# Restormer block on one core: the order of all instructions computed from other durations and margins

## The chip, the cores and the metric

The kernel runs on one core of a Trainium2 chip. A core has five engines that run side by side, each with its own in-order queue of instructions: TensorE (PE: matrix products and transposes, results into PSUM), VectorE (DVE), ScalarE (ACT), GpSimd (POOL) and SyncE (SP, which here only starts transfers). Sixteen DMA engines move data; transfers that add to what stands at their goal are started by GpSimd here. The metric is the device time of one launch in microseconds (us).

## The reference

One block of a Restormer-like network on x of shape (16, 128, 96, 96): 16 images, 128 channels, 96 x 96 pixels, float32. Attention is over channels (8 heads of 16 channels), then a feed-forward part with a 3 x 3 depthwise convolution over 512 hidden channels:

```python
x_hwc = x.transpose(0, 2, 3, 1)
xn1 = _layernorm(x_hwc, ln1_w, ln1_b)          # over the 128 channels of each pixel
q, k, v = xn1 @ wq.T, xn1 @ wk.T, xn1 @ wv.T   # split into heads, q and k l2-normed over the pixels
attn = softmax(einsum('bhcn,bhdn->bhcd', q, k) * HEAD_DIM ** -0.5)
attn_out = einsum('bhcd,bhdn->bhcn', attn, v) @ wp.T
x = x + attn_out
xn2 = _layernorm(x, ln2_w, ln2_b)
h1 = einsum('bchw,oc->bohw', xn2, w_in)        # 128 -> 512 channels
h2 = depthwise_conv_3x3(h1, w_dw)              # padding 1
h3 = gelu(h2)
x = x + einsum('bchw,oc->bohw', h3, w_out)     # 512 -> 128 channels
```

## The kernel before

**Tiles and stages.** An image is cut into 8 bands of 12 rows (`BR`), a band into 3 units of 4 rows (`UR`, 384 pixels); there are 128 bands in all. Channels lie on the 128 partitions. For each image the work goes through these stages:

1. Norm a (first layer norm, `norm(i, False, ...)`). A band of x is loaded by SP (`load`, L546 to L554). TensorE transposes four blocks of 128 pixels into one PSUM tile (`forth`, L624), VectorE takes the statistics of them (`stats`, L631, two instructions), GpSimd makes variance plus epsilon (`variance`, L638) and its power -0.5 (`power`, L642), ScalarE scales into zT (`scaled`, L678), TensorE adds the block to the Gram matrix (`gram`, L692) and transposes back (`back`, L730), and ScalarE puts the result into a ring of 144 rows in SBUF called xn (`place`, L736).
2. `attention` (L755 to L877): some fifteen small steps, from the Gram matrix to one 128 x 128 matrix that does attention and projection at once.
3. `x2` (L565 to L605): TensorE applies that matrix (`mix`, L572), ScalarE evicts (`mixed`, L581), an adding transfer by GpSimd adds x from HBM (`add_x`, L584), SP stores the sum to the output (`keep_x2`, L587).
4. Norm b (second layer norm): the same lines as norm a, with a VectorE instruction between power and scaling (`shift`, L646, it writes nb), ScalarE's scaling in L682, and without the Gram matrix.
5. `conv_job` (L884 to L972), one job for each band and chunk of 128 hidden channels: TensorE computes the hidden rows (`hidden`, L905), ScalarE copies them to h1 (`kept`, L908), VectorE does six of the eight outer taps of the convolution (`tap`, L929, some 1152 elements each, two tensors in SBUF as inputs), ScalarE makes the products of two taps (`product`, L922) and adding transfers by GpSimd put them together (`add_products`, L936), ScalarE keeps two rows for the next band (`halo`, L900) and applies GELU (L940). In 7 of 15 bands the fourth chunk's convolution is done by TensorE instead (`by_matmuls`, L994, GELU in L1000).
6. `ffn_out` (L1009 to L1056): TensorE's output product (L1018), ScalarE's eviction (L1030), and an adding transfer by GpSimd to the output (L1034); for the last two bands VectorE adds (L1025) and SP stores.

**What sets the order.** No instruction is issued where it stands in the source. Each step is given to a planner (`Plan`, L59 to L203) with `op`: its engine, its time on that engine, a place, what it reads and writes, and the time after which another engine may use its result (`result`). `Plan.order` plays all engines at once: whenever an engine is idle in its model, it takes the ready step with the smallest place whose buffers are free. Places are counted in convolution jobs and come from the loop position plus an offset for the kind of step (`at`, L346, with the table `AT`, L35; kinds that end in `_0` are image 0's). The steps are then emitted in the planned order of their starts, so this order fixes each engine's queue; on the chip only the queue's order and the waits for data and buffers remain. The planner's buffers are PSUM tiles for transposes (`tr`, 2), for products (`h`, 4 banks), for transposes back (`bk`, 1), the Gram matrix (`g`, 1), and SBUF tiles (`zT` 3, `x1` 3, `xb` 3, `pr` 5, `h3` 12).

**What the planner is told.** Times are simple formulas (L357 to L367: `t_mm`, `t_dve`, `t_act`, `t_copy`). The result of a step counts as seen by another engine after its time, a latency, and `SLACK`, 200 ns for all engines. GpSimd's variance and power are given as 1150 and 1870 ns (220 and 1010 in the early part of image 0). A transfer starts `WAIT` after its issue, or behind the transfer before it, and takes `T_ADD` (254 ns for each of 12 rows, 3048 in all) if it adds, or `T_MOVE` (133 a row, 1596) if SP starts it.

The two helpers for transfers, and the step that the planner makes of one, read:

```python
def add(p, f, r, w):
    op("POOL", 950, p, f, r, w, 1400 + SLACK, dma=T_ADD)
def move(p, f, r, w, ns):
    op("SP", 60, p, f, r, w, 900 + SLACK, dma=ns)
...
if o[8]:
    self.dma = max(time + ns + WAIT[engine], self.dma) + o[8]
    result = own = self.dma + result - time
```

## Time and profile before

| | |
|---|---|
| Median of 3 runs | 4153.88 us (4144.19 to 4156.89) |
| The profiled execution: its time | 4147.01 us |
| its span | 4145.3 us |
| TensorE's granted clock, mean | 0.997 |
| Instructions | 52245 |
| ScalarE busy | 3656.0 us (88%) |
| GpSimd busy | 2602.5 us (63%) |
| Transfers | 828.63 MB, mean 200 GB/s |

The page of a profile shows one execution: how long each engine was busy, the chain of work that ended last, and groups of equal instructions. A group's line reads: line of the code, engine, operation, what it writes <- what it reads, shapes, count | busy time in us, mean ns of one | idle time of the engine just before them, and what ended most of it. A line of waits reads: who waited <- for whom: us in total, times, longest. PEld are TensorE's weight loads, which overlap its products. A busy time is a union, so overlapping instructions count once, and the mean of one can be longer than busy time divided by count. A line of stretches gives, for each part of the span, the busy time of each engine with its number of instructions, the granted clock, the busy share of the DMA engines and what they moved. A line of transfers gives the KB of each and the median us from issue to landing.

### The profile page before, as it was taken

What the parts mean: (1) busy time and instruction counts of PE and PEld (TensorE: products, weight loads), DVE (VectorE), ACT (ScalarE), POOL (GpSimd) and SP (SyncE); (2) the same over time, 40 slices, a digit from 0 to 9 for tenths busy, and PEclk for the clock granted to TensorE, in tenths of its full rate; (3) what the DMA queues carried; (4) which work ended last, traced back from release to release, by engine and by line L of the source; (5) the groups of instructions that cost most, each with busy time, mean ns of one, the idle gap of its engine ahead of it and who ended that gap; (6) DMA issues with size and microseconds to landing.
All of it is one profiled execution on the core that took longest, in us unless ns stands there. A gap on an engine that the chain in (4) does not pass through costs nothing.

```text
span 4145.3 us, 52245 instructions
## 1 busy us (share of the span) xinstructions
PE 4060.7 (98%) x17287; PEld 2654.1 (64%) x17287; DVE 4040.2 (97%) x4446; ACT 3656.0 (88%) x7158; POOL 2602.5 (63%) x2358
## 2 busy tenths in 40 slices
PE   8999999999999999999999999999999999999999
PEld 7666666666666666666666666666666566666555
DVE  7999999999999999999999999999999999999998
ACT  5998988998989899888889889998899888999885
POOL 4767567664766656567566666766667666675442
PEclk9999999999999999999999999999999999999999
DMA  4999999999999999999999999999999899999997
GB/s 139 200 196 208 197 208 201 209 210 198 209 201 206 204 202 209 205 202 202 202 205 202 209 202 209 212 203 207 204 206 210 184 210 203 202 200 189 197 182 151
DMA packets 205519, 828.63 MB, mean 200 GB/s; under 512 B 23744, under 2 KB 25152, under 8 KB 205248
## 3 DMA queue, kind: packets, MB, share of 16 engines
q0 software_dynamic: 165744, 673.46, 84.9%
q1 hardware_dynamic: 37152, 151.01, 9.9%
q8 instruction: 138, 2.26, 0.2%
q10 hardware_dynamic: 2352, 0.81, 0.1%
q14 instruction: 133, 1.09, 0.1%
HBM read 150.03 MB, written 149.82 MB: 72 GB/s over the span
## 4 chain that ended last, share of the span: by engine, by line
PE 63%; DVE 24%; ACT 5%; DMA 4%; POOL 3%; issue 2%; POOLq 0%; ACTq 0%; DVEq 0%
DVE h L929 21%; PE h L994 17%; PE h L1018 16%; PE h L905 13%; PE g L692 4%; PE h L572 4%; PE pB_a L730 2%; PE pT_b L624 2%; PE pT_a L624 2%; PE pB_b L730 2%; DMA h<-pr 2%; DVE st_b L631 1%; DVE st_a L631 1%; ACT pr L922 1%; DMA pr<-pr 1%
## 5 line engine op out<-in xcount | busy, mean ns | idle before, releaser
L929 DVE SCALAR_TENSOR_TENSOR h<-h,ratio,h 128x1140 f32<-128x1140 f32 (+1 forms) x2257 | 3056.8, 1383 | 1.1
L922 ACT ACTIVATE pr<-h,ratio 128x1152 f32<-128x1152 f32 (+1 forms) x900 | 1153.2, 1286 | 100.6 <-DMA h<-pr 52.8
L994 PE MATMUL h<-xn,comp 128*128 128x380 f32 (+3 forms) x3324 | 1166.9, 481 | 9.2 <-ACT h L908 5.7
L1018 PE MATMUL h<-h,woutT 128*128 128x384 f32 x3072 | 1113.8, 488 | 10.8 <-ACT h L908 6.9
L905 PE MATMUL h<-xn,winT 128*128 128x384 f32 (+3 forms) x2746 | 1052.5, 490 | 15.7 <-ACT x L581 8.2
L994 PEld LDWEIGHTS h<-xn,comp 128*128 128x128 f32 x3324 | 604.4, 191 | 355.2 <-ACT h L908 8.6
L1018 PEld LDWEIGHTS h<-h,woutT 128*128 128x128 f32 x3072 | 562.0, 191 | 350.8 <-ACT h L940 12.0
L908 ACT COPY h<-h 128x384 f32<-128x384 f32 (+2 forms) x1353 | 657.0, 521 | 73.5 <-PE h L905 53.7
L936 POOL DMA_DIRECT2D pr<-pr x450 | 427.7, 950 | 435.0 <-ACT pr L922 387.0
L936 POOL DMA_DIRECT2D h<-pr x450 | 454.2, 1009 | 368.2 <-DVE h L929 153.0
L905 PEld LDWEIGHTS h<-xn,winT 128*128 128x128 f32 x2746 | 491.2, 190 | 301.8 <-issue 29.4
L929 DVE SCALAR_TENSOR_TENSOR h<-h,ratio 128x1152 f32<-128x1152 f32 x451 | 632.8, 1409 | 6.7 <-ACT h L908 6.6
L940 ACT ACTIVATE h<-h 128x1152 f32<-128x1152 f32 x453 | 546.5, 1209 | 20.4 <-DMA h<-pr 16.0
L642 POOL TENSOR_TENSOR rstd_a<-ve_a,mhalf 128x4 f32<-128x4 f32 x288 | 551.0, 1913 | 15.0
L642 POOL TENSOR_TENSOR rstd_b<-ve_b,mhalf 128x4 f32<-128x4 f32 x288 | 531.0, 1845 | 10.9
L638 POOL TENSOR_SCALAR ve_b<-st_b 128x4 f32<-128x4 f32 x288 | 329.1, 1143 | 247.8 <-DVE st_b L631 242.5
L638 POOL TENSOR_SCALAR ve_a<-st_a 128x4 f32<-128x4 f32 x288 | 330.3, 1147 | 215.4 <-DVE st_a L631 178.6
L682 ACT ACTIVATE zT<-pT_b,nb_b,rstd_b 128x128 f32<-128x128 f32 x1132 | 433.5, 492 | 31.6 <-DVE nb_b L646 29.9
L678 ACT ACTIVATE zT<-pT_a,rstd_a 128x128 f32<-128x128 f32 x1080 | 316.8, 409 | 9.5 <-POOL rstd_a L642 9.4
L692 PEld LDWEIGHTS g<-zT 128*128 128x128 f32 x2304 | 296.1, 193 | 41.3 <-issue 2.5
L572 PE MATMUL h<-xn,mwT 128*128 128x384 f32 x768 | 310.3, 490 | 7.5 <-ACT h L908 4.3
L692 PE MATMUL g<-zT 128*128 128x129 f32 x2304 | 307.5, 276 | 0.0
(172 smaller groups left out, 3675.4 us busy)
## 6 DMA issues: line engine op xcount, KB each, us to landing
h<-pr POOLq DMA_DIRECT2D x450, 576.0 KB, 8.4
pr<-pr POOLq DMA_DIRECT2D x338, 576.0 KB, 7.4
x<-in_x_dram SPq DMA_DIRECT2D x128, 576.0 KB, 6.7
out_dram<-x SPq DMA_DIRECT2D x127, 576.0 KB, 8.1
out_dram<-out POOLq DMA_DIRECT2D x126, 576.0 KB, 7.7
x<-in_x_dram POOLq DMA_DIRECT2D x125, 576.0 KB, 8.5
pr<-pr POOLq DMA_DIRECT2D x112, 528.0 KB, 7.7
out_dram<-x SPq DMA_DIRECT2D x3, 192.0 KB, 1.9
```

What stands on the lines that cost most here:

```text
L572: nc.tensor.matmul(rows(pm), lhsT=mats[i][0], rhs=interior(i, u), start=True, stop=True)
L638: nc.gpsimd.tensor_scalar(ve, d["mv"][:, :, 2], 1.0 / C, EPS, ALU.mult, ALU.add)
L642: nc.gpsimd.tensor_tensor(rstd, d["ve"], mhalf, ALU.pow)
L692: nc.tensor.matmul(grams[i][:, : P + 1], lhsT=zt[:, :P], rhs=zt, start=(q == 0 and k == 0), stop=(q == NU * TPU // QT - 1 and k == QT - 1),)
L905: nc.tensor.matmul(rows(ph)[:, k : k + m, :], lhsT=winT[:, n, :], rhs=z, start=True, stop=True)
L908: nc.scalar.copy(window(h1_, r, e - r, 1), rows(d.pop(("ph", r))))
L922: nc.scalar.activation(d["pr", t][:, o0:o1, :], shifted(t, o0, o1), AF.Copy, scale=ratio[:, n, t : t + 1])
L929: nc.vector.scalar_tensor_tensor(h3[:, o0:o1, w0:w1], shifted(t, o0, o1, w0, w1), ratio[:, n, t : t + 1], onto, ALU.mult, ALU.add)
L936: nc.gpsimd.dma_start(out=to[:, o0:o1, :], in_=d["pr", t][:, o0:o1, :], accum_op=ALU.add)
L940: nc.scalar.activation(h3, h3, AF.Gelu)
L994: nc.tensor.matmul(d["pc"][:, o0 + k : o0 + k + m, w0:w1], lhsT=comp[:, t, :], rhs=z[:, :, w0 + dx : w1 + dx], start=(t == order[0]), stop ...
L1018: nc.tensor.matmul(rows(d["po"]), lhsT=woutT[:, n, :], rhs=h3s[g, n][:, s * UR : (s + 1) * UR, :], start=(k == 0), stop=(k == NCH - 1),)
```

## The change

No step is added or taken away, and every step computes what it did. What the planner is told is changed, and with it the order of the instructions on each engine:

- All offsets in `AT` are new.
- `SLACK` becomes a table: 910 ns behind TensorE, 200 behind VectorE and ScalarE, 0 behind GpSimd's computing steps, 150 behind an adding transfer, 950 behind one that SP starts.
- Transfers: `T_ADD` 234 a row instead of 254, `T_MOVE` 121 instead of 133; `WAIT` 700 instead of 350 for GpSimd's and 1800 instead of 1300 for the others; the issue of an adding transfer takes GpSimd 800 ns instead of 950, and the latency behind a landing is 350 instead of 1400 (adding) and 900 (SP), before the margin.
- GpSimd's computing steps: variance is 250 ns and power 1010, for all images. The planner remembers until when a tap runs on VectorE (`self.two`, the tap's end plus 35 ns; only taps are marked, by `two=True`). A GpSimd computing step that starts before that time gets the rest of it added, less 143 ns. A GpSimd step that issues a transfer does not.
- The memsets of `zeros` and the table load are planned by the common helpers, at 300 and 200 ns and 1400 ns.

```diff
@@ -33,27 +33,27 @@
 LAST_ADDS = 2
 IN_TURN = ("tr", "h3", "pr", "xb", "x1")
 AT = dict(
-    load_1=-81.8, load_2=-81.05, tables=-300.65, weights=-241.6, zeros=-79.35, load_a=-132.3, forth_a=-3.95,
-    stats_a=-119.7, variance_a=57.65, power_a=43.15, scaled_a=67.75, gram=-0.3, back_a=-131.9, place_a=-4.05,
-    attention=-126.85, mix=-6.1, residual=-100.05, mixed=-72.7, add_x=-106.2, forth_b=-1.2, stats_b=-57.55,
-    variance_b=-94.65, power_b=108.15, shift_b=-68.05, scaled_b=71.3, back_b=-38.35, place_b=67.85, evicted=4.6,
-    add_out=-80.65, halo=139.4, hidden=2.8, kept=-53.4, products=2.05, add_last=-216.85, tap=8.1,
-    add_first=-80.7, gelu=650.75, conv=2.7, conv_gelu=7.9, out=6.35, add=107.4, store=112.35, mix_0=-6.7,
-    residual_0=15.25, mixed_0=37.15, add_x_0=-22.1, gram_0=6.6, forth_a_0=-278.4, forth_b_0=-3.6,
-    stats_a_0=37.95, stats_b_0=-249.6, scaled_a_0=-24.3, scaled_b_0=34.15, back_a_0=-105.15, back_b_0=-197.05,
-    place_a_0=-82.25, place_b_0=38.25, shift_b_0=0.7, late=-240.45, store_x2=23.55, store_x2_0=14.25,
-    variance_a_0=-76.6, variance_b_0=30.05, power_a_0=-132.1, power_b_0=29.1, attention_0=-126.55,
-    load_a_0=-197.15,
+    load_1=-125.15, load_2=-188.5, tables=-11.6, weights=105.75, zeros=-270.15, load_a=-127.15, forth_a=-3.95,
+    stats_a=-128.3, variance_a=70.6, power_a=-352.75, scaled_a=390, gram=0.2, back_a=-88.4, place_a=-42.05,
+    attention=-122.25, mix=-6.1, residual=-130.75, mixed=-134.85, add_x=-93.4, forth_b=-1.35, stats_b=-0.75,
+    variance_b=-212.2, power_b=50.85, shift_b=-88.2, scaled_b=99.6, back_b=-12.4, place_b=96.6, evicted=5.8,
+    add_out=-269.35, halo=538.7, hidden=2.8, kept=-49.15, products=2.05, add_last=-420.95, tap=9.15,
+    add_first=-34.25, gelu=905.05, conv=2.7, conv_gelu=8.7, out=6.35, add=-76.25, store=-175.9, mix_0=-5.4,
+    residual_0=-85.05, mixed_0=-4.8, add_x_0=56.3, gram_0=-182.1, forth_a_0=51.65, forth_b_0=-3.7,
+    stats_a_0=8.9, stats_b_0=-80.85, scaled_a_0=-176.8, scaled_b_0=1.1, back_a_0=-4.5, back_b_0=-114.85,
+    place_a_0=-35.45, place_b_0=80.15, shift_b_0=-69, late=129.95, store_x2=-48.1, store_x2_0=-109.6,
+    variance_a_0=286, variance_b_0=110.1, power_a_0=-128.05, power_b_0=15.9, attention_0=-253.7,
+    load_a_0=-278.85,
 )
 STEP = dict(scaled=0.3, hidden=0.1, products=0.5, tap=0.166, conv=1.6, conv_tap=0.03, out=0.8, out_part=0.05)
-SLACK = 200
+SLACK = dict(PE=910, DVE=200, ACT=200, POOL=0, ADD=150, MOVE=950)
 NORM1_END = 6.0
 EARLY = 5
-WAIT = dict(POOL=350, SP=1300, ACT=1300)
+WAIT = dict(POOL=700, SP=1800, ACT=1800)
 T_WEIGHTS = 3000
-T_VARIANCE = 1150
-T_POWER = 1870
-T_ADD, T_MOVE = 254 * BR, 133 * BR
+T_VARIANCE = 250
+T_POWER = 1010
+T_ADD, T_MOVE = 234 * BR, 121 * BR
 
 
 class Plan:
@@ -69,8 +69,9 @@
         self.slot = {}
         self.ops, self.writer, self.readers, self.users = [], {}, {}, {}
         self.dma = 0.0
-
-    def op(self, engine, ns, place, work, reads, writes, result, own=None, dma=0):
+        self.two = 0.0
+
+    def op(self, engine, ns, place, work, reads, writes, result, own=None, dma=0, two=False):
 
 
 
@@ -98,7 +99,7 @@
                 self.users.setdefault(t, []).append(k)
                 needs[self.users[t][0]] = True
         needs.pop(k, None)
-        self.ops.append((engine, ns, place, work, list(needs), new, result, own or result, dma))
+        self.ops.append((engine, ns, place, work, list(needs), new, result, own or result, dma, two))
 
     def order(self):
         ops, free = self.ops, self.free
@@ -162,6 +163,12 @@
             if o[8]:
                 self.dma = max(time + ns + WAIT[engine], self.dma) + o[8]
                 result = own = self.dma + result - time
+            elif engine == "POOL":
+                rest = self.two - time
+                ns, result = (ns, result) if rest <= 0 else (rest + ns - 143, rest + result - 143)
+                own = result
+            if o[9]:
+                self.two = time + ns + 35
             push(time + own, "own", k)
             push(time + ns, "idle", k)
             push(time + result, "done", k)
@@ -367,19 +374,22 @@
         return 50 + 0.832 * n
 
     def pe(ns, p, f, r, w):
-        op("PE", ns, p, f, r, w, ns + 200 + SLACK, ns)
-
-    def dve(ns, p, f, r, w):
-        op("DVE", ns, p, f, r, w, ns + 120 + SLACK, ns + 120)
+        op("PE", ns, p, f, r, w, ns + 200 + SLACK["PE"], ns)
+
+    def dve(ns, p, f, r, w, two=False):
+        op("DVE", ns, p, f, r, w, ns + 120 + SLACK["DVE"], ns + 120, two=two)
+
+    def pool(ns, p, f, r, w):
+        op("POOL", ns, p, f, r, w, ns + 33 + SLACK["POOL"])
 
     def add(p, f, r, w):
-        op("POOL", 950, p, f, r, w, 1400 + SLACK, dma=T_ADD)
+        op("POOL", 800, p, f, r, w, 350 + SLACK["ADD"], dma=T_ADD)
 
     def move(p, f, r, w, ns):
-        op("SP", 60, p, f, r, w, 900 + SLACK, dma=ns)
+        op("SP", 60, p, f, r, w, 350 + SLACK["MOVE"], dma=ns)
 
     def act(ns, p, f, r, w):
-        op("ACT", ns, p, f, r, w, ns + 150 + SLACK, ns + 150)
+        op("ACT", ns, p, f, r, w, ns + 150 + SLACK["ACT"], ns + 150)
 
     def zeros(p):
 
@@ -389,9 +399,9 @@
             nc.gpsimd.memset(t[:, r * WP :], 0.0)
 
         for t in zT_bufs:
-            op("POOL", 300, at("zeros", p - 1), lambda t=t: nc.gpsimd.memset(t[:, :, P:], 1.0), [], [("w", "ones")], 500)
+            pool(300, at("zeros", p - 1), lambda t=t: nc.gpsimd.memset(t[:, :, P:], 1.0), [], [("w", "ones")])
         for t in h1s:
-            op("POOL", 1000, at("zeros", p), lambda t=t: around(t), [], [("w", "pads")], 1200)
+            pool(300, at("zeros", p), lambda t=t: around(t), [], [("w", "pads")])
 
     def weights(p):
 
@@ -499,7 +509,7 @@
             for n in range(NCH):
                 nc.vector.tensor_scalar(v["wt"][:, n, :], v["win"][:, n, :], unit[:, n : n + 1], None, ALU.mult)
 
-        op("ACT", 1400, at("tables", p), table, [], [tables], 1500)
+        act(1400, at("tables", p), table, [], [tables])
         op("ACT", 2700, at("load_1", p), loads_1, [], [mine[1], small_1], T_WEIGHTS, dma=1000)
         op("ACT", 2300, at("load_2", p), loads_2, [], [mine[0], small_2], T_WEIGHTS, dma=1800)
         dve(1400, at("late", p), units, [small_2], [("w", "in")])
@@ -694,15 +704,14 @@
                         start=(q == 0 and k == 0), stop=(q == NU * TPU // QT - 1 and k == QT - 1),
                     )
 
-            t_variance, t_power = (T_VARIANCE, T_POWER) if not early else (220, 1010)
             trs, bt = [(key_, (name, q)) for q in qs], ("batch", (name, m))
             for q, tr in zip(qs, trs):
                 units = {t // TPU: None for t in range(q * QT, (q + 1) * QT)}
                 pe(110 * QT, at("forth" + ab, s, i), lambda q=q: forth(q), [xtok(u) for u in units], [tr])
             for j in range(QB * QT // 2):
                 dve(341, at("stats" + ab, s, i), lambda j=j: stats(j), [trs[2 * j // QT]], [bt])
-            op("POOL", t_variance, at("variance" + ab, s, i), variance, [], [bt], t_variance + 33 + SLACK)
-            op("POOL", t_power, at("power" + ab, s, i), power, [], [bt], t_power + 33 + SLACK)
+            pool(T_VARIANCE, at("variance" + ab, s, i), variance, [], [bt])
+            pool(T_POWER, at("power" + ab, s, i), power, [], [bt])
             if second:
                 dve(80, at("shift" + ab, s, i), shift, [], [bt])
             for h, (q, tr) in enumerate(zip(qs, trs)):
@@ -710,7 +719,7 @@
                 if by_dve:
                     if apart and q % 2 == 0:
                         both = [(*zt_of(k), j) for k in (q, q + 1) for j in range(2)]
-                        op("POOL", 200, at("zeros", sh), lambda q=q: zT(q), [], both, 300)
+                        pool(200, at("zeros", sh), lambda q=q: zT(q), [], both)
                     dve(by_dve * 240, at("scaled" + ab, sh, i), lambda q=q: also_scaled(q), [tr, bt], [(*zt, 0)])
                 act((QT - by_dve) * (343 if second else 250), at("scaled" + ab, sh, i), lambda q=q: scaled(q), [tr, bt], [(*zt, 1)])
                 if not second:
@@ -773,7 +782,7 @@
 
         def step(engine, ns, also=(), reads=(), writes=mine):
             def add(f):
-                op(engine, ns, s, f, [("w", "qk"), *reads], [*writes, *also], ns + 200 + SLACK)
+                op(engine, ns, s, f, [("w", "qk"), *reads], [*writes, *also], ns + 200 + SLACK[engine])
             return add
 
         wide = [("x1", ("attention", i), k) for k in range(2)]
@@ -962,7 +971,7 @@
             add(at("add_last", j), lambda t=t: add_products(t), [pr[1 + k]], [pr[0]])
         for k, t in enumerate(left):
             o0, o1 = reach(t)
-            dve(t_dve((o1 - o0) * (W if k == 0 or t % 3 == 1 else W - 1)), at("tap", j + STEP["tap"] * k), lambda t=t: tap(t), [*h1, ("w", "pads")], h3)
+            dve(t_dve((o1 - o0) * (W if k == 0 or t % 3 == 1 else W - 1)), at("tap", j + STEP["tap"] * k), lambda t=t: tap(t), [*h1, ("w", "pads")], h3, True)
         if dma_taps:
             add(at("add_first", j), lambda: add_products(dma_taps[0]), [pr[0]], h3)
         if to_halo:
```

## The prediction

> **What bounds the kernel now.** I read the head of the page first, then the chain of waits.
>
> ```profile
> span 4145.3 us, 52245 instructions
> PE 4060.7 (98%) x17287; PEld 2654.1 (64%) x17287; DVE 4040.2 (97%) x4446; ACT 3656.0 (88%) x7158; POOL 2602.5 (63%) x2358
> ...
> PE 63%; DVE 24%; ACT 5%; DMA 4%; POOL 3%; issue 2%; POOLq 0%; ACTq 0%; DVEq 0%
> ```
>
> TensorE (PE) and VectorE (DVE) both look full. To see which one cannot give way, look at the time of one instruction: taps (L929) and output products (L1018), first in the page's groups, then in the long pieces of the chain.
>
> ```profile
> L929 DVE SCALAR_TENSOR_TENSOR h<-h,ratio,h 128x1140 f32<-128x1140 f32 (+1 forms) x2257 | 3056.8, 1383 | 1.1
> L1018 PE MATMUL h<-h,woutT 128*128 128x384 f32 x3072 | 1113.8, 488 | 10.8 <-ACT h L908 6.9
> ```
> ```profile
> 4126.25 15.49 PE h L1018 x48
> ```
>
> L1018 takes 1113.8/3072 = 0.363 us of busy TensorE per instruction on the average, and 15.49/48 = 0.323 us in the last, unbroken stretch: 11% of that busy time can be squeezed. The taps have no such reserve: their records agree within the mean of 1.38 us, with 1.1 us of idle time before 2257 of them. So VectorE is the floor: 4040.2 us of work that a new order does not change, and 4145.3 - 4040.2 = 105.1 us in which it stands. (The Trainium skill, "Perfetto Trace Analysis", section "Identifying the Most-Contended Engine", says that matmul busy time misleads and weight-load time should be used; by its rule TensorE would be 64% full, not 98%, which leaves VectorE alone as the bound.) Where the 105 us lie, by stage:
>
> ```profile
> core 0: us, PE busy (x) PEld busy (x) DVE busy (x) ACT busy (x) POOL busy (x), PEclk, DMA share, GB/s
> 0.00:100.00 100.00, 86.25 (x539) 70.13 (x540) 71.22 (x193) 56.60 (x144) 46.25 (x108) 0.98 0.48 138
> 100.00:4100.00 4000.00, 3932.67 (x16618) 2559.11 (x16617) 3934.44 (x4225) 3583.53 (x6990) 2550.15 (x2244) 1.00 0.97 202
> 4100.00:4146.00 46.00, 41.73 (x133) 24.89 (x131) 34.59 (x30) 15.86 (x25) 6.08 (x7) 1.00 0.57 124
> ```
>
> 28.8 us in the first 100, 65.6 in the 4000 of the middle, and 10.7 in the 45.3 that are left. What ended the waits of the middle:
>
> ```profile
> DVE st_b L631 <- PE pT_b L624: 25.9, 31, 7.7
> DVE st_a L631 <- PE pT_a L624: 11.3, 21, 1.5
> DVE nb_b L646 <- POOL rstd_b L642: 8.3, 7, 2.0
> DVE n L828 <- PE g L822: 4.3, 8, 0.9
> DVE h L929 <- ACT h L908: 3.7, 4, 2.3
> DVE wide L800 <- ACT h L900: 2.4, 1, 2.4
> ```
>
> They are few: some 70 waits, 55.9 us in these rows. More than half is the statistics (L631) waiting for the transposes (L624). No instruction is added or removed by the change, so anything it gains comes out of these rows, the head and the tail.
>
> **The change part by part.**
>
> *Margin behind TensorE, 200 to 910 ns.* The planner now believes that another engine sees a TensorE result 0.71 us later, so statistics are put later behind their transposes, and other VectorE work (taps) in front. Without the longest wait the st_b row has 18.2 us in 30 waits, 0.61 us each, and st_a has 0.54 us each: most are shorter than the added margin. The most that it can take away is 18.2 + 11.3 + 0.7 = 30 us. It costs something too, because the planner holds PSUM banks 0.71 us longer, and TensorE already waits for banks or inputs from ScalarE:
>
> ```profile
> PE h L905 <- ACT x L581: 8.2, 9, 1.8
> PE pB_a L730 <- ACT xn L734: 7.6, 4, 6.5
> PE h L1018 <- ACT h L908: 6.9, 5, 2.9
> ```
>
> 18 such waits of another 0.71 us would be 13 us if VectorE had to follow. Between -30 and +13 I take -15: half of the gain, since the rows' mean wait is below the margin but a real delay of TensorE is not the same each time.
>
> *GpSimd's own times.* Variance and power go from fixed 1150 and 1870 ns to 250 and 1010, plus what is left of a tap that is under way, less 143 ns. The rows they must match (groups, then the record of L638 and L642):
>
> ```profile
> L642 POOL TENSOR_TENSOR rstd_a<-ve_a,mhalf 128x4 f32<-128x4 f32 x288 | 551.0, 1913 | 15.0
> L638 POOL TENSOR_SCALAR ve_a<-st_a 128x4 f32<-128x4 f32 x288 | 330.3, 1147 | 215.4 <-DVE st_a L631 178.6
> ```
> ```profile
> L638 POOL TENSOR_SCALAR ve_a<-st_a x288: 185/1262/11223, 8.0 to 3751.6; 128x4 f32<-128x4 f32 x144
> ```
> ```profile
> L642 POOL TENSOR_TENSOR rstd_a<-ve_a,mhalf x288: 996/2073/11022, 8.6 to 3753.0; 128x4 f32<-128x4 f32 x144
> ```
>
> The old constants are the means (1.147, 1.913), but with 233 ns on top; the new ones follow the pattern, a short time alone (0.185, 0.996) and about a tap more under a tap (1.262, 2.073). With a whole tap of 1.38 us left the new plan says 1.38 + 0.107 = 1.49 and 1.38 + 0.867 = 2.25 us, a little over the medians. It gains at most the 8.3 us of the nb_b row. Against it stands the maximum, 11.2 us, which no plan has:
>
> ```profile
> 3235.02 11.22 POOL L638 TENSOR_SCALAR ve_a<-st_a 128x4 f32<-128x4 f32 x1
> ```
> ```profile
> 3255.88 0.43 DVE L631 BATCH_NORM_STATS2 st_b<-pT_b 128x6 f32<-128x256 f32 x1 [7.70 <-PE pT_b L624]
> ```
> ```profile
> 3240.00:3260.00 20.00, 13.45 (x64) 9.22 (x63) 11.92 (x14) 11.64 (x25) 14.31 (x11) 0.83 0.64 124
> ```
>
> GpSimd stood there for 11.2 us, eight taps by their mean; the scaling behind it, then the PSUM buffers, then the transposes came late, and VectorE lost 20 - 11.92 = 8.1 us. One more such place is +8. I take -4, half of the row. (The Trainium skill, "SBUF — State Buffer", section "A bandwidth-pool intuition that's wrong (but worth ruling out)", has GpSimd blocked until the end of the VectorE instruction plus about 115 ns. The new planner computes much the same; by it no record would pass 1.38 + 0.115 + 0.996 = 2.5 us, and the loss at 3255 could not be. The trace has 11.2 us, so the measurement decides.)
>
> *Transfers.* One adding transfer is planned at 2808 ns of queue time instead of 3048, a plain one at 1452 instead of 1596.
>
> ```profile
> q0 software_dynamic: 165744, 673.46, 84.9%
> q1 hardware_dynamic: 37152, 151.01, 9.9%
> ...
> h<-pr POOLq DMA_DIRECT2D x450, 576.0 KB, 8.4
> pr<-pr POOLq DMA_DIRECT2D x338, 576.0 KB, 7.4
> ```
> ```profile
> 720.00:740.00 20.00, 20.00 (x85) 13.17 (x84) 19.12 (x32) 18.67 (x35) 11.63 (x11) 1.00 1.02 244
> ```
>
> Busy shares suggest the old numbers (84.9% of 4145.3 us over 450 + 450 + 125 + 126 adding transfers is 3.06 us), yet 244 GB/s have gone through in 20 us against 202 on the average: there is room, and shorter numbers are nearer. An add into an empty queue was planned to land 950 + 350 + 3048 + 1600 = 5.95 us after issue, now 800 + 700 + 2808 + 500 = 4.81; the medians are 7.4 and 8.4, so products that came later than planned already are now expected 1.1 us earlier still. Who waits for them is ScalarE:
>
> ```profile
> ACT pr L922 <- DMA h<-pr: 52.8, 51, 7.5
> ACT pr L922 <- DMA pr<-pr: 31.3, 33, 2.6
> ```
>
> 84 waits by 1.1 us are 92 us there, covered by its 4000 - 3583.5 = 416 us of idle time. Queued behind such a wait are the copies of L908, for which VectorE now waits 3.7 us; were the cover gone for a quarter, +23. On the other side -6 (the rows of L908 and L900). I take -2. SP's transfers, with a margin of 950 ns, load x or store x2 far ahead; no VectorE row waits for them: nothing.
>
> *Places of the preparation.* Weight transposes ("weights", "late") go from -241.6 and -240.45 to +105.75 and +129.95, behind image 1's first norm. The head has 28.8 us of VectorE gaps to put them into, so they may free up to 6; if they hold up attention of image 0 instead, the statistics that go ahead of them are work that would come anyway: at most four bands (the ring's 48 spare rows), 18 statistics of 0.43 us, +8. I take 0. The tail's last 15.49 us on TensorE are the last band's products, in the same dependencies: 0.
>
> Sum: 4145.3 - 15 - 4 - 2 = 4124 us of span. The profiled run took 4147.0, 1.7 more than its span: 4126 us. That run is 6.9 below the median of 4153.9; I leave the forecast at 4126, since 6.9 is less than the 0.3% (12 us) that a measurement can tell.
>
> **The rivals.**
>
> *Most waits go.* If the new order removes all of the waits in the six VectorE rows: 4145.3 - 55.9 + 1.7 = 4091 us. For it: they are few and short, and TensorE and transfers have the reserve shown. Against: 8 of the 25.9 us come from the stuck GpSimd instruction.
>
> *The change doesn't do what it says.* Real times scatter (L638 from 0.185 to 11.2 us), so after some microseconds the engines run by their waits and not by the plan; as many stalls arise in other places: 4147 us, 4135 to 4160.
>
> *Slower: GpSimd starved behind longer runs of taps.* Norm b's statistics lose their head start: stats_b from -57.55 to -0.75 jobs, while taps go from 8.1 to 9.15. Old taps may now run ahead of new statistics; runs of taps without a break grow longer, and a GpSimd variance in them is stuck as at 3235, now with no transposed tile in reserve. GpSimd's margin of 0 takes away what covered it. Queued behind the stuck instruction are the DMA issues of the products, and ScalarE and the PSUM buffers wait for those. The price is 8.1 us for a place; from four new places on it outweighs my -21 and the 12 us of the measurement, and eight give 4124 + 65 + 1.7 = 4191 us. Against: of the four records of L638 and L642 over 6 us (first and last below), one cost this much. (By the skill's rule above this rival could not happen at all; with the trace's 11.2 us it keeps its chance.)
>
> ```profile
> 177.41 6.08 POOL L642 TENSOR_TENSOR rstd_a<-ve_a,mhalf 128x4 f32<-128x4 f32 x1
> ```
> ```profile
> 3352.05 7.20 POOL L638 TENSOR_SCALAR ve_a<-st_a 128x4 f32<-128x4 f32 x1
> ```
>
> **How the numbers follow.** Forecast 4126, own range 4105 to 4141: chance 0.45. Most waits go: 0.17. No effect: 0.13. Starved GpSimd or another loss of its size: 0.25. Faster by over 0.3% (below 4141) is 0.45 + 0.17 + 0.01 from the edge of no effect = 0.63, within it 0.12, slower (above 4166) 0.25. The range reaches down to 4088 and up to 4182, which leaves out about half of the slower case and a little below: 2 in 10.
>
> **What would show it.** Right: the rows of L631 waiting for L624 fall from 37 us to about 22, nb_b to about 4, VectorE's busy time in the middle of the run rises from 98.4 to about 98.9%, its total stays at 4040 within 10. GpSimd's step is wrong if the maxima of L638 and L642 recur in more than four places over 6 us. The transfer step is wrong if L929 waiting for L908 passes 10 us. If TensorE's waits for ScalarE double, the margin has cost more than it gave. The whole is wrong if VectorE's busy total itself moves.

## The result, and the profile after

The changed kernel takes 4295.8 us (median of 6 runs, 4289.6 to 4303.1) against 4149.0 (4134.5 to 4159.2) for the kernel before on the same chip: a ratio of 1.0354, with a 95% interval of 1.033 to 1.0378. The prediction said 4126 us, 4088 to 4182. It was wrong in sign and outside its range.

The head of the page and the chain, after:

```profile
span 4297.0 us, 52138 instructions
PE 4121.2 (96%) x17287; PEld 2645.6 (62%) x17287; DVE 4050.6 (94%) x4446; ACT 3653.8 (85%) x7158; POOL 2508.2 (58%) x2358
...
DMA 8%; DVE 6%; PE 5%; ACT 4%; POOL 3%; issue 2%; POOLq 0%; ACTq 0%; DVEq 0%
```

(Lines have moved down by nine or ten: the taps are L938, ScalarE's products L931, its copies to h1 L917, its GELU L949, GpSimd's adds L945, its variance and power L648 and L652, the transposes L634, the statistics L641, nb L656.) VectorE's work is 4050.6 us, 10 more than before; its idle time went from 105 to 4297.0 - 4050.6 = 246 us. The chain is followed back only over the last 28% of the span. There it no longer runs mostly through TensorE: landings of transfers are its largest part, 8 of the 28%. By stage:

```profile
0.00:100.00 100.00, 81.08 (x503) 64.27 (x504) 65.92 (x188) 49.38 (x127) 43.05 (x105) 0.97 0.39 118
100.00:4100.00 4000.00, 3850.45 (x16164) 2469.29 (x16163) 3803.97 (x4102) 3473.68 (x6816) 2405.19 (x2191) 0.99 0.94 196
4100.00:4297.00 197.00, 189.64 (x623) 112.02 (x621) 180.69 (x157) 130.75 (x216) 59.98 (x63) 1.00 0.81 161
```

The loss is spread over the whole middle: 196 us of idle VectorE in 4000 us instead of 65.6; the head gives 34.1 instead of 28.8. What VectorE waits for, from 100 to 4250 us (who <- for whom: us in total, times, longest):

```profile
DVE nb_b L656 <- POOL rstd_b L652: 86.4, 89, 2.3
DVE st_a L641 <- PE pT_a L634: 48.4, 50, 5.8
DVE st_b L641 <- PE pT_b L634: 30.6, 40, 4.2
DVE h L938 <- ACT h L917: 10.4, 9, 3.3
```

and what ScalarE waits for (the third L922 row of the kernel before, then four rows of the changed kernel):

```profile
ACT pr L922 <- DMA out_dram<-out: 14.9, 12, 2.8
...
ACT pr L931 <- DMA h<-pr: 161.1, 127, 6.5
ACT pr L931 <- DMA pr<-pr: 114.3, 97, 3.4
ACT pr L931 <- DMA out_dram<-out: 57.7, 52, 3.2
ACT h L949 <- DMA h<-pr: 57.1, 40, 3.0
```

Two readings offer themselves. GpSimd's results come too late for VectorE (8.3 to 86.4 us), where the margin was set to 0. Or transfers come too late for ScalarE (the products: 52.8 + 31.3 + 14.9 = 99.0 us before, 161.1 + 114.3 + 57.7 = 333.1 now), where landings were planned earlier. Yet the transfers themselves are not slower (transfers: count, KB, median us from issue to landing):

```profile
h<-pr POOLq DMA_DIRECT2D x450, 576.0 KB, 7.7
pr<-pr POOLq DMA_DIRECT2D x338, 576.0 KB, 7.0
...
out_dram<-out POOLq DMA_DIRECT2D x126, 576.0 KB, 7.1
x<-in_x_dram POOLq DMA_DIRECT2D x125, 576.0 KB, 8.0
```

8.4 and 7.4 us stood in the first two rows before. A stretch of the changed kernel shows a way on which a late transfer can reach VectorE (start us, us, engine, line; in brackets how long the engine stood before it, and for whom):

```profile
3199.75 1.17 ACT L949 ACTIVATE h<-h 128x1152 f32<-128x1152 f32 x1 [0.98 <-DMA h<-pr]
...
3203.97 1.29 ACT L931 ACTIVATE pr<-h,ratio 128x1152 f32<-128x1152 f32 x1
...
3206.59 0.42 ACT L909 COPY h<-h 128x192 f32<-128x192 f32 x1
...
3207.52 0.88 POOL L945 DMA_DIRECT2D pr<-pr  x1 [1.09 <-ACT h L909]
...
3208.09 1.21 POOL L594 DMA_DIRECT2D x<-in_x_dram  x1
...
3208.65 1.75 POOL L652 TENSOR_TENSOR rstd_b<-ve_b,mhalf 128x4 f32<-128x4 f32 x1
...
3210.43 0.16 DVE L656 SCALAR_TENSOR_TENSOR nb_b<-st_b,rstd_b 128x4 f32<-128x4 f32 x1 [0.59 <-POOL rstd_b L652]
...
3210.80 1.25 ACT L931 ACTIVATE pr<-h,ratio 128x1152 f32<-128x1152 f32 x1 [1.23 <-DMA out_dram<-out]
```

At 3199.75 ScalarE has stood 0.98 us for a sum to land, and from there it works without a gap. Behind it GpSimd, with the issue of an add in its queue, has stood 1.09 us for ScalarE at 3207.52. The power of norm b is queued behind two issues, and at 3210.43 VectorE has stood 0.59 us for it. At 3210.80 ScalarE has again stood for a transfer, 1.23 us, too late to have caused that. The links between these waits are read from the queues' order. So one lateness can make both readings, and only runs tell which is the cause.

### The profile page after: what moved, and what is told of

Read it like the earlier page. It is cut to its first block, busy times and chain, and to the rows that moved or that the text cites. A ratio compares the mean times of both kernels' runs of the same rounds, so it can differ in the third digit from the quotient of the medians.

```text
span 4297.0 us, 52138 instructions
## 1 busy us (share of the span) xinstructions
PE 4121.2 (96%) x17287; PEld 2645.6 (62%) x17287; DVE 4050.6 (94%) x4446; ACT 3653.8 (85%) x7158; POOL 2508.2 (58%) x2358
## 3 DMA queue, kind: packets, MB, share of 16 engines
q0 software_dynamic: 165744, 673.46, 82.1%
## 5 line engine op out<-in xcount | busy, mean ns | idle before, releaser
L938 DVE SCALAR_TENSOR_TENSOR h<-h,ratio,h 128x1140 f32<-128x1140 f32 (+1 forms) x2257 | 3061.1, 1383 | 2.0
L931 ACT ACTIVATE pr<-h,ratio 128x1152 f32<-128x1152 f32 (+1 forms) x900 | 1140.6, 1277 | 337.9 <-DMA h<-pr 161.1
L1027 PE MATMUL h<-h,woutT 128*128 128x384 f32 x3072 | 1128.6, 492 | 35.7 <-ACT out L1039 13.6
L945 POOL DMA_DIRECT2D pr<-pr x450 | 413.7, 919 | 711.8 <-ACT pr L931 588.2
L945 POOL DMA_DIRECT2D h<-pr x450 | 448.7, 998 | 439.9 <-DVE h L938 184.1
L914 PEld LDWEIGHTS h<-xn,winT 128*128 128x128 f32 x2746 | 488.1, 190 | 336.0 <-ACT h L917 31.3
L917 ACT COPY h<-h 128x384 f32<-128x384 f32 (+2 forms) x1353 | 659.4, 520 | 38.3 <-PE h L914 33.3
L938 DVE SCALAR_TENSOR_TENSOR h<-h,ratio 128x1152 f32<-128x1152 f32 x451 | 633.7, 1409 | 13.9 <-ACT h L917 13.8
L949 ACT ACTIVATE h<-h 128x1152 f32<-128x1152 f32 x453 | 543.2, 1201 | 72.0 <-DMA h<-pr 62.4
L652 POOL TENSOR_TENSOR rstd_a<-ve_a,mhalf 128x4 f32<-128x4 f32 x288 | 521.1, 1810 | 20.4
L652 POOL TENSOR_TENSOR rstd_b<-ve_b,mhalf 128x4 f32<-128x4 f32 x288 | 510.5, 1778 | 17.2
L648 POOL TENSOR_SCALAR ve_a<-st_a 128x4 f32<-128x4 f32 x288 | 308.2, 1070 | 180.1 <-DVE st_a L641 155.7
L648 POOL TENSOR_SCALAR ve_b<-st_b 128x4 f32<-128x4 f32 x288 | 295.5, 1026 | 151.1 <-DVE st_b L641 150.3
```

What stands on the lines that cost most here:

```text
L648: nc.gpsimd.tensor_scalar(ve, d["mv"][:, :, 2], 1.0 / C, EPS, ALU.mult, ALU.add)
L652: nc.gpsimd.tensor_tensor(rstd, d["ve"], mhalf, ALU.pow)
L914: nc.tensor.matmul(rows(ph)[:, k : k + m, :], lhsT=winT[:, n, :], rhs=z, start=True, stop=True)
L917: nc.scalar.copy(window(h1_, r, e - r, 1), rows(d.pop(("ph", r))))
L931: nc.scalar.activation(d["pr", t][:, o0:o1, :], shifted(t, o0, o1), AF.Copy, scale=ratio[:, n, t : t + 1])
L938: nc.vector.scalar_tensor_tensor(h3[:, o0:o1, w0:w1], shifted(t, o0, o1, w0, w1), ratio[:, n, t : t + 1], onto, ALU.mult, ALU.add)
```

## The experiments

All ratios are to the kernel before, run on the same chip (4119 to 4149 us on the five occasions; so ratios are compared, not times), with 95% intervals. "Plan" is the planner's own mean time from issue to landing over the 1151 adding transfers, counted in its model of each order until the planner lets another engine use the sum; the latency and margin behind the landing are in it (1.6 us of the 8.7 before, 0.5 us of the 6.5 in the changed kernel). It is no measured time. "Chip" is the mean of the rows of median times to landing, weighted by their counts (changed kernel: (450 x 7.7 + 338 x 7.0 + 112 x 7.3 + 126 x 7.1 + 125 x 8.0) / 1151 = 7.4 us). The column for L931 adds the three rows of ScalarE's products waiting for transfers (L922 in the kernel before, e1 and e8, L927 in e11).

| Run | ratio | plan | chip | L931 for transfers, us | nb_b for GpSimd, us |
|---|---|---|---|---|---|
| before | 1 | 8.7 | 8.0 | 99 | 8 |
| changed | 1.0354 (1.033 to 1.0378) | 6.5 | 7.4 | 333 | 86 |
| e1 old durations and margin, new offsets | 1.0026 (1.0015 to 1.0036) | 8.9 | 7.9 | 69 | 6 |
| e2 new durations and margins, old offsets | 1.0351 (1.0327 to 1.0375) | 6.6 | 7.5 | 264 | 63 |
| e3 changed, GpSimd margin 600 | 1.0437 (1.0404 to 1.047) | 6.5 | 7.4 | 286 | 44 |
| e4 changed, old adds | 1.0016 (1.0004 to 1.0028) | 8.5 | 7.8 | 129 | 19 |
| e5 changed, landing +1.1 us | 1.0147 (1.0124 to 1.0171) | 7.6 | 7.7 | 230 | 64 |
| e6 changed, 3048 ns an add | 1.0073 (1.0047 to 1.01) | 7.9 | 7.7 | 166 | 39 |
| e7 changed, issue 950 ns | 1.0345 (1.0317 to 1.0374) | 6.6 | 7.4 | 266 | 65 |
| e8 before, new adds | 1.0341 (1.0316 to 1.0366) | 6.5 | 7.4 | 262 | 21 |
| e9 e4, TensorE margin 200 | 1.003 (1.0017 to 1.0044) | 8.7 | 7.8 | 94 | 26 |
| e10 e4, GpSimd margin 200 | 1.0034 (1.0017 to 1.0052) | 8.6 | 7.9 | 156 | 37 |
| e11 e4, old GpSimd times | 1.0012 (0.9997 to 1.0027) | 8.6 | 7.9 | 109 | 14 |
| e12 e4, landing +0.6 us | 0.998 (0.9963 to 0.9998) | 9.3 | 8.1 | 86 | 29 |
| e13 changed, pr<-pr +1.1 us | 1.0293 (1.0276 to 1.0311) | 7.1 | 7.5 | 220 | 53 |
| e14 changed, h<-pr +1.1 us | 1.0301 (1.0279 to 1.0323) | 7.0 | 7.5 | 220 | 57 |
| e15 changed, x and out +1.1 us | 1.0482 (1.0453 to 1.0512) | 6.7 | 7.4 | 319 | 89 |
| e16 changed, nudge | 1.0385 (1.0365 to 1.0406) | 6.5 | 7.4 | 285 | 64 |

**Offsets or numbers (e1, e2).** e1 is the kernel before with the new table `AT` and nothing else; e2 is the changed kernel with the old table.

```diff
 e1, on the kernel before:
-    load_1=-81.8, load_2=-81.05, tables=-300.65, weights=-241.6, zeros=-79.35, load_a=-132.3, forth_a=-3.95,
+    load_1=-125.15, load_2=-188.5, tables=-11.6, weights=105.75, zeros=-270.15, load_a=-127.15, forth_a=-3.95,
...
 e2, on the changed kernel:
-    load_1=-125.15, load_2=-188.5, tables=-11.6, weights=105.75, zeros=-270.15, load_a=-127.15, forth_a=-3.95,
+    load_1=-81.8, load_2=-81.05, tables=-300.65, weights=-241.6, zeros=-79.35, load_a=-132.3, forth_a=-3.95,
...
```

> The kernel before with the new offsets alone: its own durations and its one margin of 200 ns. If the durations and margins lose the time (theory M), the new offsets on the old durations come out near the kernel before, 4150 +- 30 us, with nb_b waiting for rstd_b about 10 us. If the offsets themselves lose it (theory P), it stays near 4296 us. If any pair of offsets and durations that do not belong together is bad (theory F), it lies well above 4296 us.

> The changed kernel with the old offsets: new durations and margins alone. Theory M: near 4296 us, nb_b waiting for rstd_b above 60 us. Theory P: near 4150 us. Theory F: well above 4296 us too.

Theory M holds on both sides: 1.0026 and 1.0351. The new offsets (61 of the 67 differ; forth_a, mix, hidden, products, conv and out keep theirs) move the time by 0.26%; the durations and margins make all the rest, with either table.

**GpSimd's margin (e3).**

```diff
-SLACK = dict(PE=910, DVE=200, ACT=200, POOL=0, ADD=150, MOVE=950)
+SLACK = dict(PE=910, DVE=200, ACT=200, POOL=600, ADD=150, MOVE=950)
```

> The changed kernel with a margin of 600 ns instead of 0 behind each GpSimd computing step, so 1.2 us over variance and power. Theory M: nb_b's wait falls from 86 us to below 20 us and the time by as much, to about 4225 us. Theory P or F: the wait moves or falls, and the time changes by less than 25 us.

A miss, and an instructive one: the time was to fall to about 4225 us, and the ratio rose from 1.0354 to 1.0437. VectorE's rows of e3:

```profile
DVE st_a L641 <- PE pT_a L634: 58.7, 59, 5.0
DVE st_b L641 <- PE pT_b L634: 51.6, 56, 4.0
DVE nb_b L656 <- POOL rstd_b L652: 43.8, 57, 1.7
DVE h L938 <- ACT h L917: 25.6, 22, 4.7
```

The wait for GpSimd halves, as margin should make it, but those for the transposes and for ScalarE grow by 31 and 15 us. With e4, the next run, this says that the longest row of the changed kernel was a place where lateness showed, not where it began.

**The adds' numbers (e4).**

```diff
-        op("POOL", 800, p, f, r, w, 350 + SLACK["ADD"], dma=T_ADD)
+        op("POOL", 950, p, f, r, w, 1400 + 200, dma=T_ADD)
-WAIT = dict(POOL=700, SP=1800, ACT=1800)
+WAIT = dict(POOL=350, SP=1800, ACT=1800)
-T_ADD, T_MOVE = 234 * BR, 121 * BR
+T_ADD, T_MOVE = 254 * BR, 121 * BR
```

> The changed kernel with the old numbers for adding transfers alone (950 ns of GpSimd, start 350 ns later, 3048 ns each, landing seen 1600 ns later). Theory M with the transfers as its main part: ScalarE's waits for transfers before L931 fall from 333 us to about 100 us, the statistics' waits for the transposes from 79 us to about 40 us, and the time to about 4230 us. If GpSimd's margin is the main part: ScalarE's waits fall, the time by less than 25 us.

It goes further than the theory that asked for it, which had about 4230 us: the ratio is 1.0016, nearly all of the loss. GpSimd's margin is still 0 in e4, and its new times, the new offsets and the new numbers for SP's transfers stand, yet nb_b waits 19 us instead of 86. The rows of e4:

```profile
DVE nb_b L656 <- POOL rstd_b L652: 19.3, 23, 1.2
...
DVE h L938 <- ACT h L917: 3.3, 4, 1.6
...
DVE st_a L641 <- PE pT_a L634: 1.8, 3, 1.3
DVE st_b L641 <- PE pT_b L634: 1.2, 4, 0.4
```
```profile
ACT pr L931 <- DMA h<-pr: 86.4, 83, 3.8
...
ACT pr L931 <- DMA pr<-pr: 28.3, 40, 2.9
```

Note the last two rows of VectorE: the waits for the transposes are 3 us, against 37 before the change. TensorE's margin of 910 ns may do this, once the adds no longer cover it up; but the new offsets alone (e1) had 8.8 + 6.1 = 15 us, and e9 below tries the margin.

**Which of the adds' numbers (e5 to e8).** One number is put back at a time, and in e8 the new ones are put into the kernel before.

```diff
 e5, on the changed kernel:
-SLACK = dict(PE=910, DVE=200, ACT=200, POOL=0, ADD=150, MOVE=950)
+SLACK = dict(PE=910, DVE=200, ACT=200, POOL=0, ADD=1250, MOVE=950)
 e6, on the changed kernel:
-T_ADD, T_MOVE = 234 * BR, 121 * BR
+T_ADD, T_MOVE = 254 * BR, 121 * BR
 e7, on the changed kernel:
-        op("POOL", 800, p, f, r, w, 350 + SLACK["ADD"], dma=T_ADD)
+        op("POOL", 950, p, f, r, w, 350 + SLACK["ADD"], dma=T_ADD)
 e8, on the kernel before:
-T_ADD, T_MOVE = 254 * BR, 133 * BR
+T_ADD, T_MOVE = 234 * BR, 133 * BR
-WAIT = dict(POOL=350, SP=1300, ACT=1300)
+WAIT = dict(POOL=700, SP=1300, ACT=1300)
-        op("POOL", 950, p, f, r, w, 1400 + SLACK, dma=T_ADD)
+        op("POOL", 800, p, f, r, w, 350 + 150, dma=T_ADD)
```

> The changed kernel with the landing of an adding transfer seen 1.1 us later (ADD 1250 instead of 150), its 2808 ns in the queue and GpSimd's 800 ns left. Theory L (what costs is that the plan has the sums landing earlier than they do; the plan's own mean from issue to landing is 6.5 us in the changed kernel, 8.5 in e4, and this run's is 7.6): about half of the loss comes back, 4180 to 4230 us, ScalarE's waits for transfers before L931 fall to 200 us or below. Theory Q (what costs is that the plan's queue of transfers is emptier than the chip's, so that too many are issued at a time): near 4296 us. Theory G (GpSimd's time of an issue): near 4296 us.

> The changed kernel with 3048 ns for an adding transfer in the queue instead of 2808, nothing else. The plan's mean from issue to landing becomes 7.9 us. Theory L: 4160 to 4210 us. Theory Q: 4120 to 4150 us, as e4. Theory G: near 4296 us.

> The changed kernel with 950 ns of GpSimd for the issue of an adding transfer instead of 800, nothing else. The plan's mean from issue to landing stays at 6.6 us. Theory L and Q: 4280 to 4310 us. Theory G: below 4200 us, with nb_b waiting for rstd_b below 30 us.

> The kernel before with the new numbers for adding transfers alone (GpSimd 800 ns, start 700 ns later, 2808 ns in the queue, landing seen 500 ns later instead of 1600), its offsets, margins and GpSimd's computing times left. The plan's mean from issue to landing falls from 8.7 to 6.5 us. If these numbers alone make the loss: 4240 to 4310 us, ScalarE's waits for transfers before its products above 250 us. If they lose only together with the margins or GpSimd's new times: below 4180 us.

The times of all four fall where theory L put them: 1.0147 (4205 us) and 1.0073 (4174 us) for e5 and e6, 1.0345 (4287 us) for e7, 1.0341 (4282 us) for e8. One part of it missed: in e5 ScalarE's products wait 230 us for transfers, where 200 or less was expected. Neither the rate (e6) nor the constant behind a landing (e5) is special, each gives back part; `WAIT` was not tried alone. Ordered by the plan's landing, 6.5, 7.6, 7.9 and 8.5 us, the ratios are 1.0354, 1.0147, 1.0073 and 1.0016, while the chip takes 7.4 to 7.8 us throughout. The loss fades step by step, and not at the point where plan and chip agree: e6's plan is already 0.2 us later than the chip on the average and still loses 0.73%. e8 shows that the numbers need no other part of the change. There the lateness shows elsewhere (who <- for whom, e8, lines of the kernel before):

```profile
DVE st_a L631 <- PE pT_a L624: 79.1, 96, 5.7
DVE st_b L631 <- PE pT_b L624: 71.5, 85, 4.2
DVE nb_b L646 <- POOL rstd_b L642: 21.3, 23, 2.4
```
```profile
ACT pr L922 <- DMA h<-pr: 151.2, 147, 4.3
ACT pr L922 <- DMA pr<-pr: 82.5, 89, 2.9
```

Here the same loss comes through the transposes (151 us) and hardly through GpSimd (21 us). With the same offsets and the new margins and GpSimd times (e2) it is 67 and 63 us: they move the place at which VectorE feels the loss, and which of them does was not tried. ScalarE's products wait alike in both, 262 and 264 us.

**The rest of the change, with the adds mended (e9 to e12).**

```diff
 e9, on e4:
-SLACK = dict(PE=910, DVE=200, ACT=200, POOL=0, ADD=150, MOVE=950)
+SLACK = dict(PE=200, DVE=200, ACT=200, POOL=0, ADD=150, MOVE=950)
 e10, on e4:
-SLACK = dict(PE=910, DVE=200, ACT=200, POOL=0, ADD=150, MOVE=950)
+SLACK = dict(PE=910, DVE=200, ACT=200, POOL=200, ADD=150, MOVE=950)
 e11, on e4:
-SLACK = dict(PE=910, DVE=200, ACT=200, POOL=0, ADD=150, MOVE=950)
+SLACK = dict(PE=910, DVE=200, ACT=200, POOL=200, ADD=150, MOVE=950)
-T_VARIANCE = 250
-T_POWER = 1010
+T_VARIANCE = 1150
+T_POWER = 1870
-            elif engine == "POOL":
-                rest = self.two - time
-                ns, result = (ns, result) if rest <= 0 else (rest + ns - 143, rest + result - 143)
-                own = result
 e12, on e4:
-        op("POOL", 950, p, f, r, w, 1400 + 200, dma=T_ADD)
+        op("POOL", 950, p, f, r, w, 1400 + 800, dma=T_ADD)
```

> e4 (the changed kernel with the old numbers for adding transfers) with TensorE's margin back at 200 ns. If that margin is worth the 15 us that the prediction gave it: 0.2 to 0.5% over e4's ratio of 1.0016, and the statistics' waits for the transposes go from e4's 3 us to 20 us or more. If it is worth nothing: within 0.2% of e4 whatever these waits do. If holding the PSUM banks longer cost more: below e4's ratio by 0.2% or more.

> e4 with 200 ns instead of 0 behind each GpSimd computing step. If the margin of 0 still costs: nb_b's wait for rstd_b falls from 19 us to below 8 us and the ratio to 0.995 to 0.999, faster than both. If not: the wait falls and the ratio stays within 0.2% of e4's 1.0016.

> e4 with GpSimd's computing times as before too: 1150 and 1870 ns, margin 200 ns, no rest of a tap. Left of the change are the offsets, the other margins, and SP's transfers. If GpSimd's measured times help (the prediction gave them 4 us): the ratio rises by 0.1 to 0.3%. If they hurt, since the tail of GpSimd's times is longer than a tap: the ratio falls below 1.000.

> e4 with the landing of an adding transfer seen 600 ns later still; the plan's mean from issue to landing becomes 9.3 us, over the 7.6 to 8.1 us that the traces show. Theory L says that once the plan is no earlier than the chip nothing more comes of it: ratio 0.998 to 1.004. If lateness pays without end: 0.99 to 0.997. If too late a landing costs as much as too early a one: above 1.008.

e9: the waits for the transposes come back (25 us), as expected, but the ratio is only 0.14% above e4's, about 6 us, with intervals that overlap. e10 is a miss: nb_b waits longer (37 us), not shorter, and nothing is gained. The profiles of e9 and e10 hold something that e4's does not, one GpSimd step that stands through a run of taps, and behind it one long stand of VectorE (e9, then e10):

```profile
602.82 10.97 POOL L652 TENSOR_TENSOR rstd_a<-ve_a,mhalf 128x4 f32<-128x4 f32 x1
627.56 0.43 DVE L641 BATCH_NORM_STATS2 st_b<-pT_b 128x6 f32<-128x256 f32 x1 [8.71 <-PE pT_b L634]
```
```profile
1463.89 15.78 POOL L648 TENSOR_SCALAR ve_a<-st_a 128x4 f32<-128x4 f32 x1 [0.91 <-DVE st_a L641]
1490.44 0.43 DVE L641 BATCH_NORM_STATS2 st_b<-pT_b 128x6 f32<-128x256 f32 x1 [10.83 <-PE pT_b L634]
```

8.71 and 10.83 us are more than the 6 and 7 us by which e9 and e10 lie above e4, so these two ratios say little about the margins. e11: that GpSimd's measured times are worth anything is not shown; its ratio is within 0.04% of e4's, with wide overlap, and neither of the two outcomes named came. e12: a plan that is 1.2 us later than the chip costs nothing. 0.998 is the only ratio under 1; its interval (0.9963 to 0.9998) reaches from theory L's range into that of its rival, and so small a difference between two orders can be chance.

**Which transfers, and how much is shuffling (e13 to e16).**

```diff
 e13 to e15, on the changed kernel (late=1100 for one kind of add):
-    def add(p, f, r, w):
-        op("POOL", 800, p, f, r, w, 350 + SLACK["ADD"], dma=T_ADD)
+    def add(p, f, r, w, late=0):
+        op("POOL", 800, p, f, r, w, 350 + SLACK["ADD"] + late, dma=T_ADD)
 e16, on the changed kernel:
-SLACK = dict(PE=910, DVE=200, ACT=200, POOL=0, ADD=150, MOVE=950)
+SLACK = dict(PE=920, DVE=200, ACT=200, POOL=0, ADD=150, MOVE=950)
```

> The changed kernel with a landing seen 1.1 us later for the add of one product to the other alone (pr<-pr, 450 of 1151 adding transfers). e5, all of them 1.1 us later, took 2.0% off. If each transfer counts alike (theory L): 0.6 to 1.0% less than the changed kernel, 4250 to 4270 us. If this kind carries the loss, since the next add, the reuse of its buffer and GpSimd's queue hang on it: 4200 to 4230 us. If it carries none: above 4280 us.

> The same for the add of the products to the taps' sum alone (h<-pr, 450), behind which GELU and the output products wait. Alike: 4250 to 4270 us. If this kind carries the loss: 4200 to 4230 us, with L949's waits for h<-pr below 30 us. If none: above 4280 us.

> The same for the adds of x and to the output alone (251). Alike: 4265 to 4285 us. If this kind carries the loss: 4200 to 4230 us. If none: above 4290 us.

> The changed kernel with TensorE's margin at 920 ns instead of 910, which says nothing new to the planner and only shuffles its choices. If a shuffle by itself moves the time little: 4280 to 4310 us. If plans are so touchy that the runs above could be chance: more than 40 us from the changed kernel.

The nudge moves the ratio by 0.3% (the intervals just overlap), so a difference of 0.3% between two orders says nothing, and those of e1, e4 and e9 to e12 among each other hardly more. e13 and e14 take 0.6% and 0.5% off; an equal share of e5's 2.0% for 450 of 1151 transfers would be 0.8%. e15 was expected to help a little and came out 1.3% worse, outside what every theory named. The three parts together come to no gain at all, where all transfers at once (e5) gave 2.0%: that each transfer counts alike is not borne out, and why e15 loses is left open. It bounds how far a single plan can be read. The adds' numbers as a whole stand above this: the six orders with planned landings at 6.5 or 6.6 us (changed, e2, e3, e7, e8, e16) lie at 1.034 to 1.044, the six with 8.5 us or more (e1, e4, e9 to e12) at 0.998 to 1.003.

## Why the prediction was wrong, step by step

**What bounds the kernel: right.** VectorE's work nearly stayed (4040.2 and 4050.6 us; the 10.4 us more are just beyond the 10 that the prediction allowed), and 141 us of the loss are idle time of it: in the 4000 us of the middle it is 95.1% busy, where 98.9% was forecast. Also right: TensorE's 98% was no bound. It had the same work to do in the slower kernel and showed 4121.2 us busy.

**The step that failed: transfers, "I take -2".** Two things went wrong in it. First, the sentence that "products that came later than planned already are now expected 1.1 us earlier still". The 5.95 us set against the medians of 7.4 and 8.4 were the plan's landing in an empty queue, while the medians hold the time in the queue. With its own queue the old plan had the sums usable after 8.7 us on the average, later than the chip's landings at 8.0. The new plan has 6.5, earlier than the chip's 7.4. So on the average products did not come later than planned before the change, as that sentence has it; the change took the plan from the late side to the early one, and e4 to e6 show that the loss goes with it. Whether 2808 or 3048 ns is nearer the chip's own rate is not shown: 244 GB/s in the stretch that was quoted speaks for the shorter, while the transfers' share of the changed kernel's span, 82.1% of 4297.0 us over 1151 adds, is 3.07 us each.

```profile
q0 software_dynamic: 165744, 673.46, 82.1%
```

Second, the cover. "84 waits by 1.1 us are 92 us there, covered by its 4000 - 3583.5 = 416 us of idle time." ScalarE's waits for the products grew by more, 333.1 - 99.0 = 234 us, and were not covered: VectorE's idle time grew by 246 - 105 = 141 us with them, and it shrank with them in e4. Idle time of an in-order queue is no store that a wait can be paid from. It lies where ScalarE waits for others, and behind each new wait stand the scaling of zT, the copies to h1 and the products whose adds GpSimd must issue. The bound of +23 for "the cover gone for a quarter" was only the row of L908, which did rise by 6.7 us (3.7 to 10.4), past the 10 us that the prediction had named as the sign of a wrong transfer step. The paths that the term left out were GpSimd's queue (nb_b, +78 us) and the PSUM tiles that ScalarE frees for the transposes (79.0 - 37.2 = +42 us; what TensorE itself stands for ScalarE's scaling before its transposes rose from 32.7 to 61.3 us). With the row of L908 they make 127 of the 141 us of added idle time.

**Margin behind TensorE: mechanism right, worth not shown.** The prediction gave it up to 30 us of the waits for the transposes. In e4 they fall by 34 us, and in e9 they come back to 25, of which 8.7 stand behind the GpSimd step shown there. The time differs by 0.14%, about 6 us, with overlapping intervals and less than the 0.3% of the nudge: the -15 us are neither shown nor excluded.

**GpSimd's own times: no effect shown.** Predicted -4; e11 against e4 is 0.04%, and 4 us would be 0.1%. The wait that the prediction named as its gain rose from 8.3 to 86.4 us in the changed kernel, but as a consequence of the adds; in e4 it is 19.

**Places: nearly nothing.** Predicted 0 with +8 at most; e1 has 0.26%, 11 us, no more than the nudge. The head gave away 71.22 - 65.92 = 5.3 us of VectorE's work, and that goes with the offsets (64.90 us in e1's first 100 us, 69.12 in e2's); which of them does it was not tried.

**The rival that came out slower fell too.** "GpSimd starved behind longer runs of taps" had the right sign and the wrong cause. Its price of 8.1 us for a place was about right (5.8 us in the changed kernel, 8.7 and 10.8 in e9 and e10), but in the changed kernel such records grew fewer (L648 and L652: min/median/max ns):

```profile
L648 POOL TENSOR_SCALAR ve_a<-st_a x288: 184/1247/11128, 7.9 to 3896.1; 128x4 f32<-128x4 f32 x144
L648 POOL TENSOR_SCALAR ve_b<-st_b x288: 184/1172/2217, 72.0 to 4189.3; 128x4 f32<-128x4 f32 x144
```
```profile
L652 POOL TENSOR_TENSOR rstd_a<-ve_a,mhalf x288: 1006/2075/2494, 8.2 to 3897.0; 128x4 f32<-128x4 f32 x144
L652 POOL TENSOR_TENSOR rstd_b<-ve_b,mhalf x288: 1005/2057/3693, 72.3 to 4190.9; 128x4 f32<-128x4 f32 x144
```

One record over 6 us is left of four, and the medians have hardly moved.

## What to carry to other kernels

When an order is computed, a modelled transfer that lands too early costs more than one that lands too late: 0.9 us too early on some 7.4 came with 3.5% here, 1.2 us too late cost nothing. Equal averages are not enough: with the plan 0.2 us later than the chip 0.7% was still lost, with 0.7 us later 0.2%. A transfer's rate is not its landing time; compare the model's distribution from issue to landing, queue included, with the profile's before using either. And the longest wait of the engine that bounds the kernel need not be where the lateness begins: follow the queue of the engine it waits for, and try the repair at both ends.

## What the runs showed that was not expected

GpSimd's small instructions mostly enter when the tap under way ends (medians of 1.2 to 1.3 us for work of 0.18 us alone), but now and then one stands much longer through a whole run of taps: 11.1 and 11.2 us at most in the changed kernel and the one before, 15.8 in e10; the longest in e4 is 3.4 us. The Trainium skill, "SBUF — State Buffer", section "A bandwidth-pool intuition that's wrong (but worth ruling out)", has GpSimd blocked until the end of the VectorE instruction plus about 115 ns, measured there on a transfer's issue beside a VectorE copy: the medians agree with it, these records do not. What sets them apart was not tried. One such record is worth as much as the differences between good plans. An order that differs only in a margin of 10 ns in 910 moved the ratio by 0.3%, and one that differed in the landing of 251 transfers moved it by 1.3% to the wrong side: plans for engines that are 97 and 98% full are touchy, and a single plan is a sample of one.
